# The rest of a low-rank product, repeated to 128 columns so that a gate's rows need no DRAM relay

## The chip, the cores and the metric

The kernel runs on one core of a Trainium2 chip. The metric is the device time of one execution in microseconds, as the median of several runs. The core has a matrix engine (TensorE, PE in the profile, with its weight loads shown as PEld), a vector engine (VectorE, DVE), a scalar engine (ScalarE, ACT), a general engine (GpSimd, POOL) and a queue processor (SyncE, SP) that issues all DMAs of this kernel. Each engine works through its own list of instructions in order and waits for others at semaphores.

## The reference

The reference is a transformer layer with self attention, cross attention and a feed-forward part, followed by one RWKV layer (time mixing with a recurrent state, then channel mixing). The input has 16 sequences of 256 tokens with 512 channels, all in float32. The change lies at the start of the time mixing:

```
xa = _ln(x, ln1_w, ln1_b)
sx = shift(xa) - xa
xxx = xa + sx * maa_x
t = tanh(xxx @ maa_w1).reshape(B, L, 5, 32)
m = einsum('blfd,fdc->blfc', t, maa_w2)
xw, xk, xv, xr, xg = (xa + sx * (maa_j + m[:, :, j]) for the five j)
```

`maa_w1` has 512 rows and 160 columns, which is five groups of 32. Each group of 32 tanh values is multiplied by its own 32 x 512 matrix, and the result blends the token with its predecessor, once for each of five uses: decay (w), key (k), value (v), receptance (r) and gate (g). The gate is the fifth.

## The kernel before

The kernel works in stages: self attention (A), cross attention (B), and then, for the sequences 0 to 7 and again for 8 to 15, a feed-forward stage (C) and a mix stage (D). The recurrence inside groups of eight tokens (I) runs beside the later stages, and the tail (E) carries the state, makes the outputs and does the channel mixing. One batch is one sequence of 256 tokens.

**The order.** The program is not issued as written. Each operation is recorded with the engine or engines that may do it, an assumed cost, and the tiles that it reads and writes (`emit`, `dma`). A list scheduler (`Sched.run`) then simulates engines with these costs, always takes the operation that could start first (ties by a priority made of the recording order and the table `PRIO`), and picks one of the allowed engines. So a small edit can change the order and the engine of operations far away. All DMAs are issued by SP, in the order found. Tiles live in a common pool: 34 slots of 4 KB per partition, each of which can hold one large tile or two small ones, and 4 blocks of 16 KB. For each stage `SIZES` says how many tiles of a tag may live at once, and tiles of one tag are given out in the order of recording. In the mix stage `xj`, the tiles of the blends, has three.

**Precise products.** Float32 values are split into a rounded part ("hi") and the remainder ("lo") by `split`: one copy by ScalarE or VectorE and one subtraction by VectorE or GpSimd. A large product is three matmuls per step: hi x hi, hi x lo and lo x hi (`mm3`, lines 486 to 488). The small product with `maa_w2` needs only one matmul, because the three terms are stacked along the contraction: 98 rows are 32 rows of hi, 32 of lo, 32 of hi again and two rows of ones that bring in `maa_j`. The weights `W2[j]` are stacked to match.

**The mix of one batch** (`mix`). `front` normalises, transposes and makes `xa`, `sx` and the first blend `xx`. `tmix` multiplies `xx` with `maa_w1`: 128 columns with the weights `W1` and the last 32 with `W1b`, 12 matmuls each, into the two halves of one PSUM bank. ScalarE applies tanh to both (line 1025), and both are split into the tile `th`. Now the 32 rows of each group, which stand in different partitions, have to be brought into partitions 0 to 97. This is done through DRAM, by the relay tensor `tdr`: two writes for the first four groups, one for the fifth, and then two reads into `S5` (four groups) and two into `S5b` (the fifth). The rows of ones are put into `tdr` once, in `mix_weights`. `blend(b, j)` then multiplies `W2[j]` with `S5` or, for j = 4, with `S5b` (line 1045), multiplies by `sx`, adds `xa` (lines 1050 and 1051) and splits the result into two `xj` tiles (lines 557 and 558). From these, `decay`, `rates`, `project` and `gate` make the five outputs. The recording order has `front` and `tmix` of the next batch beside the first two blends of this one, so the five groups of a batch are made most of a batch ahead of their use.

In `decay`, a similar stacked operand is made without DRAM: the weights `dw1` hold the 64 columns twice, so the product stands twice in 128 partitions, and the upper half is replaced by the remainder.

Of the kernel before, what the change touches and what calls it, by code (L numbers as in the profile page):

```python
# [9 lines left out]
F32R = mybir.dt.float32r  # L10
AF = mybir.ActivationFunctionType
# [9 lines left out]
def fv(ap):  # L21

    return ap.bitcast(F32)
# [368 lines left out]
class Kern:  # L392
# [505 lines left out]
class Rec(Kern):  # L898
# [14 lines left out]
    def mix_weights(self):  # L913

        nc, I, tile = self.nc, self.I, self.tile
        W1, W1b, dw1 = tile("W1", [128, 4, 2, 128], "W1", F32R), tile("W1b", [128, 4, 2, 32], "W1b", F32R), tile("dw1", [128, 4, 2, 128], "dw1", F32R)
# [14 lines left out]
        st, lo = tile("st", [128, 512], "st"), tile("st", [66, 512], "st2", F32R)  # L931
# [10 lines left out]
        self.tdr, self.t2l = [], []  # L942
        o1, o2 = tile("st", [66, 256], "ones"), tile("st", [66, 256], "ones2", F32R)
        self.dma(o1, lambda: o1[64:66], lambda: I["c_ones"], 2048)
        self.emit("DVE", c_dve(256), lambda: nc.vector.tensor_copy(out=o2[64:66], in_=o1[64:66]), [o1], [o2])
        for i in range(2):
            h = self.relay("tdr", [66, 5, 256], "tdr")
            self.dma(None, lambda h=h: h[64:66], lambda: fv(o2[64:66]).unsqueeze(1).to_broadcast([2, 5, 256]), 10240, r=[o2], w=[(h, 3)])
# [51 lines left out]
    def mix(self, src, rsrc, out, W, bs=range(B), side=None):  # L1000

        nc, tile, emit = self.nc, self.tile, self.emit
        W1, W1b, W2, dw1, D1, D2 = self.mixw
        st = {}
# [11 lines left out]
        def tmix(b):  # L1016
            xa, sx, xx = st[b]
            pt = tile("p_p", [128, 2, 256], "pt")
            xs = [lambda k=k: self.two(xx, k) for k in range(4)]
            self.mm3((pt, 0), lambda: pt[:, 0, :], [lambda k=k: (W1[:, k, 0, :], W1[:, k, 1, :]) for k in range(4)], xs, 256, [W1] + xx)  # L1020
            self.mm3((pt, 1), lambda: pt[0:32, 1, :], [lambda k=k: (W1b[:, k, 0, :], W1b[:, k, 1, :]) for k in range(4)], xs, 256, [W1b] + xx)
            T, th = tile("T", [128, 2, 256], "tt"), tile("xj", [128, 2, 2, 256], "th", F32R)
            dr, S5, S5b = self.tdr[b % 2], tile("S5", [98, 4, 256], "S5", F32R), tile("S5b", [98, 256], "S5b", F32R)
            for i, p in ((0, 128), (1, 32)):
                emit("ACT", c_act(256), lambda i=i, p=p: nc.scalar.activation(out=T[0:p, i, :], in_=pt[0:p, i, :], func=AF.Tanh), [(pt, i)], [(T, i)])
                self.split(256, lambda i=i, p=p: T[0:p, i, :], lambda i=i, p=p: th[0:p, i, 1, :], lambda i=i, p=p: th[0:p, i, 0, :], [(T, i)], (th, (i, 1)), (th, (i, 0)))
            for x in range(2):
                self.dma(None, lambda x=x: dr[32 * x : 32 * x + 32, 0:4, :].rearrange("d j n -> j d n"), lambda x=x: fv(th[:, 0, x, :]), 131072, [(th, (0, x))], [(dr, x)])
            self.dma(None, lambda: dr[0:64, 4, :].rearrange("(x d) n -> d x n", x=2), lambda: fv(th[0:32, 1, :, :]), 65536, [(th, (1, 0)), (th, (1, 1))], [(dr, 2)])
            self.dma(None, lambda: fv(S5[0:32]), lambda: dr[32:64, 0:4, :], 131072, [(dr, 1)], [(S5, 0)])  # L1030
            self.dma(None, lambda: fv(S5[32:98]), lambda: dr[0:66, 0:4, :], 66 * 4096, [(dr, 0), (dr, 1), (dr, 3)], [(S5, 1)])
# [85 lines left out]
        for i in range(5 * first, 5 * end):  # L1117
            b, j = divmod(i, 5)
# [115 lines left out]
class Tail(Rec):  # L1234
# [306 lines left out]
    "D": dict(wb=16, row=2, sm=4, st=4, x=1, xa=4, xx=2, W1=1, W1b=1, W2=5, dw1=1, dw2=2, t2l=2, T=3, xj=3, S5=2, S5b=2, s1=1, o=3, p_p=2, p_s=3, p_t=3, tdr=2),  # L1541
# [106 lines left out]
```

## Time and profile before

| what | us |
|---|---|
| median of 3 runs (lowest, highest) | 3563.89 (3561.29, 3566.48) |
| the profiled execution, its own time | 3571.95 |
| its span in the profile | 3570.2 |
| TensorE busy | 3273.7 |
| VectorE busy | 2843.3 |
| ScalarE busy | 1882.5 |
| GpSimd busy | 1395.8 |

The span runs from the first to the last instruction of the profiled execution. "Busy" counts the time in which an engine executes instructions; the ends of matmuls are modelled, so a busy TensorE need not be at its peak. Windows of the trace give the busy time of each engine in a stretch, and the clock that TensorE was granted there (1.00 is full). A row of the waits reads "who waited, for whose instruction": the engine, the tile it was about to write and the line, then the engine, tile and line that released it. Tiles from the common pool appear as slot, block or bank; buffers of the relay as tdr. A line can be that of a helper that many places call: 486 to 488 are all precise products, 472 all subtractions of `split` and `sub`, 461 all DMAs. The first mix stage is at about 1815 to 2140 us, the second at about 2460 to 2780 us, and the tail is from there to the end.

### The profile page before, as it was taken

The page shows a single profiled execution, that of the slowest core. Times are in us where ns is not written, and L with a number is a line of the kernel's source. Part 1 is how long each engine was busy: PE and PEld are TensorE (multiplying, and loading weights), DVE is VectorE, ACT ScalarE, POOL GpSimd, SP SyncE. Part 2 cuts the span into 40 slices and gives each one's busy share as a digit, 9 for nine tenths or more (in the row PEclk, how much of TensorE's full clock was granted, in tenths as well). Part 3 has the DMA queues.
Part 4 walks back from the last instruction along what each step waited for, and adds up shares of the span by engine and source line. Part 5 has one row for each costly group of instructions (what it writes and reads, how often), then busy time and mean ns, then how long its engine had stood idle before and what let it go on. Part 6 is the DMA issues. An engine that isn't in the chain of part 4 may idle for free. (4 is left out here: it accounts for less than half of the span.)

```text
span 3570.2 us, 72760 instructions
## 1 busy us (share of the span) xinstructions
PE 3273.7 (92%) x26978; PEld 2620.6 (73%) x26978; DVE 2843.3 (80%) x6696; ACT 1882.5 (53%) x4722; POOL 1395.8 (39%) x1853
## 2 busy tenths in 40 slices
PE   6999999989999999899999989999999558878899
PEld 4777877767777777788887879998787445555555
DVE  6888898868887788766788788899878688887653
ACT  4665666656666666433354454344444565554532
POOL 3444444444444444100021129994211476764110
PEclk9999999999999999899999999999999789998999
DMA  3111000021111110300134463343444877674420
GB/s 97 37 31 35 27 25 31 21 90 46 43 43 43 43 51 25 100 25 24 42 111 134 131 203 110 112 138 107 129 144 156 245 206 205 182 217 127 133 81 24
DMA packets 325051, 336.83 MB, mean 94 GB/s; under 512 B 40978, under 2 KB 228446, under 8 KB 324698
## 3 DMA queue, kind: packets, MB, share of 16 engines
q1 hardware_dynamic: 324698, 332.18, 30.5%
q8 instruction: 214, 3.51, 0.4%
q14 instruction: 139, 1.14, 0.1%
HBM read 199.92 MB, written 132.16 MB: 93 GB/s over the span
## 5 line engine op out<-in xcount | busy, mean ns | idle before, releaser
L721 POOL TENSOR_SCALAR slot<-slot,k_rin 128x256 f32<-128x256 f32 x1024 | 482.0, 488 | 691.8 <-DVE k_rin L718 624.8
L472 POOL TENSOR_TENSOR slot<-slot,slot 128x512 f32<-128x512 f32 (+9 forms) x394 | 540.4, 1393 | 312.7 <-ACT slot L551 133.2
L715 ACT ACTIVATE slot<-slot,k_nmx 128x256 f32<-128x256 f32 x1024 | 507.9, 498 | 199.3 <-DVE k_nmx L714 168.8
L486 PE MATMUL bank<-slot,block 128*128 128x256 f32 x1792 | 510.9, 285 | 0.2 <-ACT slot L467 0.2
L487 PE MATMUL bank<-slot,block 128*128 128x256 f32 x1792 | 508.0, 284 | 0.3 <-DVE slot L603 0.3
L488 PE MATMUL bank<-slot,block 128*128 128x256 f32 x1792 | 507.9, 283 | 0.0
L467 ACT ACTIVATE slot<-bank 128x512 f32<-128x512 f32 (+2 forms) x659 | 351.5, 565 | 270.4 <-PE bank L488 142.8
L486 PE MATMUL bank<-block,slot 128*128 128x512 f32 x1152 | 468.4, 407 | 11.3 <-ACT slot L557 10.2
L488 PE MATMUL bank<-block,slot 128*128 128x512 f32 x1152 | 453.8, 394 | 9.0 <-DVE slot L558 9.0
L487 PE MATMUL bank<-block,slot 128*128 128x512 f32 x1152 | 452.5, 393 | 0.0
L714 DVE CUSTOM_DVE_ANT_0 slot<-slot,slot 128x256 f32<-128x256 f32 x998 | 390.9, 436 | 0.0
L708 DVE SCALAR_TENSOR_TENSOR slot<-bank,slot 128x512 f32<-128x512 f32 x512 | 329.9, 680 | 44.3 <-PE bank L746 21.0
L1471 PE MATMUL bank<-block,slot 128*128 128x512 f32 x768 | 354.4, 613 | 1.6 <-DVE slot L1517 1.0
L486 PEld LDWEIGHTS bank<-slot,block 128*128 128x128 f32 x1792 | 344.1, 192 | 10.3 <-ACT slot L467 2.3
L487 PEld LDWEIGHTS bank<-slot,block 128*128 128x128 f32 x1792 | 344.0, 192 | 5.3 <-DVE slot L603 0.5
L488 PEld LDWEIGHTS bank<-slot,block 128*128 128x128 f32 x1792 | 344.1, 192 | 0.0
L487 PE MATMUL bank<-slot,slot 128*128 128x256 f32 (+2 forms) x960 | 309.1, 322 | 12.4 <-DVE slot L472 9.7
L486 PE MATMUL bank<-slot,slot 128*128 128x256 f32 (+2 forms) x960 | 307.9, 321 | 10.4 <-ACT slot L551 9.3
L734 PE MATMUL bank<-k_c,slot 128*128 128x128 f32 x2048 | 287.5, 281 | 25.1 <-POOL slot L721 10.9
L488 PE MATMUL bank<-slot,slot 128*128 128x256 f32 (+2 forms) x960 | 306.1, 319 | 1.5 <-DVE slot L558 1.5
L734 PEld LDWEIGHTS bank<-k_c,slot 128*128 128x128 f32 x2048 | 232.1, 143 | 96.3 <-POOL slot L721 64.1
L1471 PEld LDWEIGHTS bank<-block,slot 128*128 128x128 f32 x768 | 146.0, 196 | 168.6 <-issue 156.5
(195 smaller groups left out, 6639.3 us busy)
## 6 DMA issues: line engine op xcount, KB each, us to landing
slot<-in SPq DMA_DIRECT2D x153, 256.0 KB
slot<-x SPq DMA_DIRECT2D x64, 512.0 KB
x<-slot SPq DMA_DIRECT2D x48, 512.0 KB
slot<-in SPq DMA_DIRECT2D x32, 512.0 KB
sdr<-slot SPq DMA_DIRECT2D x128, 128.0 KB
slot<-sdr SPq DMA_DIRECT2D x32, 512.0 KB
s_k<-slot SPq DMA_DIRECT2D x16, 512.0 KB
s_w<-slot SPq DMA_DIRECT2D x16, 512.0 KB
```

Of the source, the lines that this page charges most:

```text
L467: self.emit(("ACT", "DVE"), (c_act(n), c_dve(n)), (lambda: nc.scalar.activation(out=out(), in_=in_(), func=AF.Copy), lambda: nc.vector.ten ...
L472: self.emit(("DVE", "POOL"), (c_dve(n), c_pool(n)), (lambda: nc.vector.tensor_tensor(out=out(), in0=in0(), in1=in1(), op=op), lambda: nc.g ...
L486: nc.tensor.matmul(o, lhsT=lh, rhs=rh, start=first and i == 0, stop=False)
L487: nc.tensor.matmul(o, lhsT=lh, rhs=rl, start=False, stop=False)
L488: nc.tensor.matmul(o, lhsT=ll, rhs=rh, start=False, stop=last and i == k - 1)
L708: emit("DVE", c_dve(512), lambda j=j, T=T: nc.vector.scalar_tensor_tensor(out=T(), in0=ps[j](), scalar=-scale, in1=mask(), op0=ALU.mult, o ...
L714: emit("DVE", c_dve(256) + 80, lambda T=T, j=j, qt=qt: nc.vector.tensor_tensor_reduce(out=T[:, qt, :], in0=T[:, qt, :], in1=negb[:, qt, :] ...
L715: emit("ACT", c_act(256, 1, 1), lambda T=T, Et=Et, j=j, qt=qt: nc.scalar.activation(out=Et[:, qt, :], in_=T[:, qt, :], func=AF.Exp, scale= ...
L721: emit("POOL", 470, lambda jj=jj, qt=qt: nc.gpsimd.tensor_scalar(out=E[jj][:, qt, :], in0=E[jj][:, qt, :], scalar1=rin[:, qt, jj : jj + 1] ...
L734: nc.tensor.transpose(pt[:, k, 128 * qt : 128 * qt + 128], E[j][:, qt, 128 * k : 128 * k + 128], self.ident())
L1471: self.nc.tensor.matmul(po(), lhsT=x[k // 2][:, k % 2, ts], rhs=w[k // 2][:, k % 2, :], start=k == 0, stop=k == 3)
```

## The change

The weights of the last 32 columns, `W1b`, become 128 columns wide and hold the 32 columns four times. The product then stands four times in 128 partitions. Tanh is taken on 96 of them. One copy brings all 96 rows, rounded, into `S5b`, and one subtraction overwrites rows 32 to 63 with the remainder. The rows of ones are written once into two lasting `S5b` tiles, `t4`. The write of the fifth group to `tdr` and its two reads go, and `tdr` has four groups in place of five. The tanh tile `th` now holds only the first 128 rows; it is half as large and has the tag `s1`, of which there are two in place of one, and no longer the tag `xj`.

```diff
-        W1, W1b, dw1 = tile("W1", [128, 4, 2, 128], "W1", F32R), tile("W1b", [128, 4, 2, 32], "W1b", F32R), ...
+        W1, W1b, dw1 = tile("W1", [128, 4, 2, 128], "W1", F32R), tile("W1b", [128, 4, 2, 128], "W1b", F32R), ...
...
-                self.split(4 * m, lambda st=st, o=o, m=m: st[:, :, o : o + m], lambda w=w: w[:, :, 0, :], lambda w=w: w[:, :, 1, :], [st], (w, 0), (w, 1))
+                rows = lambda w, x, m=m: w[:, :, x, :].rearrange("p k (r c) -> p k r c", c=m)
+                self.split(512, lambda st=st, o=o, m=m: st[:, :, o : o + m].unsqueeze(2).to_broadcast([128, 4, 128 // m, m]), lambda w=w, rows=rows: rows(w, 0), lambda w=w, rows=rows: rows(w, 1), [st], (w, 0), (w, 1))
...
+        o3 = tile("st", [98, 256], "ones3")
+        self.dma(o3, lambda: o3[96:98], lambda: I["c_ones"], 2048)
...
-            h = self.relay("tdr", [66, 5, 256], "tdr")
+            h = self.relay("tdr", [66, 4, 256], "tdr")
...
+            h = tile("S5b", [98, 256], f"S5b{i}", F32R)
+            self.emit("DVE", c_dve(256), lambda h=h: nc.vector.tensor_copy(out=h[96:98], in_=o3[96:98]), [o3], [(h, 2)])
+            self.t4.append(h)
...
-            self.mm3((pt, 1), lambda: pt[0:32, 1, :], [lambda k=k: (W1b[:, k, 0, :], W1b[:, k, 1, :]) for k in range(4)], xs, 256, [W1b] + xx)
-            T, th = tile("T", [128, 2, 256], "tt"), tile("xj", [128, 2, 2, 256], "th", F32R)
-            dr, S5, S5b = self.tdr[b % 2], tile("S5", [98, 4, 256], "S5", F32R), tile("S5b", [98, 256], "S5b", F32R)
-            for i, p in ((0, 128), (1, 32)):
+            self.mm3((pt, 1), lambda: pt[:, 1, :], [lambda k=k: (W1b[:, k, 0, :], W1b[:, k, 1, :]) for k in range(4)], xs, 256, [W1b] + xx)
+            T, th = tile("T", [128, 2, 256], "tt"), tile("s1", [128, 2, 256], "th", F32R)
+            dr, S5, S5b = self.tdr[b % 2], tile("S5", [98, 4, 256], "S5", F32R), self.t4[b % 2]
+            for i, p in ((0, 128), (1, 96)):
                 emit("ACT", c_act(256), lambda i=i, p=p: nc.scalar.activation(out=T[0:p, i, :], in_=pt[0:p, i, :], func=AF.Tanh), [(pt, i)], [(T, i)])
-                self.split(256, lambda i=i, p=p: T[0:p, i, :], lambda i=i, p=p: th[0:p, i, 1, :], lambda i=i, p=p: th[0:p, i, 0, :], [(T, i)], (th, (i, 1)), (th, (i, 0)))
+            self.split(256, lambda: T[:, 0, :], lambda: th[:, 1, :], lambda: th[:, 0, :], [(T, 0)], (th, 1), (th, 0))
...
-            self.dma(None, lambda: dr[0:64, 4, :].rearrange("(x d) n -> d x n", x=2), lambda: fv(th[0:32, 1, :, :]), 65536, [(th, (1, 0)), (th, (1, 1))], [(dr, 2)])
...
-            self.dma(None, lambda: fv(S5b[0:32]), lambda: dr[32:64, 4, :], 32768, [(dr, 2)], [(S5b, 0)])
-            self.dma(None, lambda: fv(S5b[32:98]), lambda: dr[0:66, 4, :], 66 * 1024, [(dr, 2), (dr, 3)], [(S5b, 1)])
+            emit(("ACT", "DVE"), (c_act(256) + 43, c_dve(256, 0, True)), (lambda: nc.scalar.activation(out=S5b[0:96], in_=T[0:96, 1, :], func=AF.Copy), lambda: nc.vector.tensor_copy(out=S5b[0:96], in_=T[0:96, 1, :])), [(T, 1)], [(S5b, 0), (S5b, 1)])
+            self.sub(256, lambda: S5b[32:64], lambda: T[32:64, 1, :], lambda: fv(S5b[32:64]), [(T, 1), (S5b, 0)], [(S5b, 1)])
...
-    "D": dict(..., S5=2, S5b=2, s1=1, ...),
+    "D": dict(..., S5=2, S5b=2, s1=2, ...),
```

More of the change, by code (lines that the diff above doesn't have):

```diff
@@ L915, in mix_weights @@
         nc, I, tile = self.nc, self.I, self.tile
-        W1, W1b, dw1 = tile("W1", [128, 4, 2, 128], "W1", F32R), tile("W1b", [128, 4, 2, 32], "W1b", F32R), tile("dw1", [128, 4, 2, 128], "dw1", F32R)
+        W1, W1b, dw1 = tile("W1", [128, 4, 2, 128], "W1", F32R), tile("W1b", [128, 4, 2, 128], "W1b", F32R), tile("dw1", [128, 4, 2, 128], "dw1", F32R)
         for src, n, ws in ((I["L1_xattn_maa_w1"], 160, ((W1, 0, 128), (W1b, 128, 32))), (I["c_dw1"], 128, ((dw1, 0, 128),))):
@@ L941, in mix_weights @@
         self.mixw = W1, W1b, W2, dw1, D1, D2
-        self.tdr, self.t2l = [], []
+        self.tdr, self.t2l, self.t4 = [], [], []
+        o3 = tile("st", [98, 256], "ones3")
+        self.dma(o3, lambda: o3[96:98], lambda: I["c_ones"], 2048)
         o1, o2 = tile("st", [66, 256], "ones"), tile("st", [66, 256], "ones2", F32R)
@@ L946, in mix_weights @@
         for i in range(2):
-            h = self.relay("tdr", [66, 5, 256], "tdr")
-            self.dma(None, lambda h=h: h[64:66], lambda: fv(o2[64:66]).unsqueeze(1).to_broadcast([2, 5, 256]), 10240, r=[o2], w=[(h, 3)])
+            h = self.relay("tdr", [66, 4, 256], "tdr")
+            self.dma(None, lambda h=h: h[64:66], lambda: fv(o2[64:66]).unsqueeze(1).to_broadcast([2, 4, 256]), 8192, r=[o2], w=[(h, 3)])
             self.tdr.append(h)
@@ L1027, in tmix @@
             for x in range(2):
-                self.dma(None, lambda x=x: dr[32 * x : 32 * x + 32, 0:4, :].rearrange("d j n -> j d n"), lambda x=x: fv(th[:, 0, x, :]), 131072, [(th, (0, x))], [(dr, x)])
-            self.dma(None, lambda: dr[0:64, 4, :].rearrange("(x d) n -> d x n", x=2), lambda: fv(th[0:32, 1, :, :]), 65536, [(th, (1, 0)), (th, (1, 1))], [(dr, 2)])
-            self.dma(None, lambda: fv(S5[0:32]), lambda: dr[32:64, 0:4, :], 131072, [(dr, 1)], [(S5, 0)])
-            self.dma(None, lambda: fv(S5[32:98]), lambda: dr[0:66, 0:4, :], 66 * 4096, [(dr, 0), (dr, 1), (dr, 3)], [(S5, 1)])
@@ L1032, in tmix @@
-            self.dma(None, lambda: fv(S5b[0:32]), lambda: dr[32:64, 4, :], 32768, [(dr, 2)], [(S5b, 0)])
-            self.dma(None, lambda: fv(S5b[32:98]), lambda: dr[0:66, 4, :], 66 * 1024, [(dr, 2), (dr, 3)], [(S5b, 1)])
+                self.dma(None, lambda x=x: dr[32 * x : 32 * x + 32, :, :].rearrange("d j n -> j d n"), lambda x=x: fv(th[:, x, :]), 131072, [(th, x)], [(dr, x)])
+            emit(("ACT", "DVE"), (c_act(256) + 43, c_dve(256, 0, True)), (lambda: nc.scalar.activation(out=S5b[0:96], in_=T[0:96, 1, :], func=AF.Copy), lambda: nc.vector.tensor_copy(out=S5b[0:96], in_=T[0:96, 1, :])), [(T, 1)], [(S5b, 0), (S5b, 1)])
@@ L1034, in tmix @@
+            self.sub(256, lambda: S5b[32:64], lambda: T[32:64, 1, :], lambda: fv(S5b[32:64]), [(T, 1), (S5b, 0)], [(S5b, 1)])
+            self.dma(None, lambda: fv(S5[0:32]), lambda: dr[32:64], 131072, [(dr, 1)], [(S5, 0)])
+            self.dma(None, lambda: fv(S5[32:98]), lambda: dr[0:66], 66 * 4096, [(dr, 0), (dr, 1), (dr, 3)], [(S5, 1)])
             st[b][2] = S5, S5b
@@ L1540 @@
     "C": dict(wb=16, w=16, row=2, cf=1, sm=4, st=8, x=2, xh=2, xT=2, E=4, PT=1, cT=1, p_p=2, p_s=3, p_t=3),
-    "D": dict(wb=16, row=2, sm=4, st=4, x=1, xa=4, xx=2, W1=1, W1b=1, W2=5, dw1=1, dw2=2, t2l=2, T=3, xj=3, S5=2, S5b=2, s1=1, o=3, p_p=2, p_s=3, p_t=3, tdr=2),
+    "D": dict(wb=16, row=2, sm=4, st=4, x=1, xa=4, xx=2, W1=1, W1b=1, W2=5, dw1=1, dw2=2, t2l=2, T=3, xj=3, S5=2, S5b=2, s1=2, o=3, p_p=2, p_s=3, p_t=3, tdr=2),
     "E": dict(wb=8, sm=4, st=2, x=3, xx=8, T=4, T4=2, s0=2, Y=2, rp=1, gt=1, uc=2, d0=2, Sc=2, tot=1, gs=2, KB=3, KBc=1, SBc=1, SB=4, VO=2, RP=4, p_p=2, p_u=2, p_y=2, p_t=2, d_s=2),
```

## The prediction

> **What bounds the kernel now.** I read the page's head first, then TensorE's idle time by stage (windows), then its waits in the two mix stages, one batch of the mix in order of time, and last the tail stage.
>
> ```profile
> span 3570.2 us, 72760 instructions
> PE 3273.7 (92%) x26978; PEld 2620.6 (73%) x26978; DVE 2843.3 (80%) x6696; ACT 1882.5 (53%) x4722; POOL 1395.8 (39%) x1853
> PE   6999999989999999899999989999999558878899
> ```
>
> TensorE is busy for 92% of the span, so most stages end when its matmuls do. The slices with 5 and 8 (from about 2760 us) are the tail. The mix runs twice, at 1815 to 2140 and at 2460 to 2780 us. Ten-microsecond windows of one batch of it (PE, PEld, DVE, ACT, POOL busy, then clock and DMA):
>
> ```profile
> 1930.00:1940.00 10.00, 10.00 (x75) 9.53 (x74) 5.17 (x8) 3.64 (x7) 0.00 (x0) 1.00 0.48 146
> 1940.00:1950.00 10.00, 7.26 (x44) 5.76 (x43) 9.90 (x19) 4.88 (x10) 3.64 (x5) 0.94 0.16 54
> 1950.00:1960.00 10.00, 10.00 (x49) 8.32 (x48) 7.95 (x18) 6.13 (x12) 1.63 (x2) 0.89 0.23 63
> ```
>
> A batch alternates: a stretch bound by TensorE (10.00, VectorE only 5.17), then one bound by VectorE (9.90), in which TensorE loses 2.74 us and the granted clock falls for a moment (0.94, then 0.89). What TensorE waits for in the first mix stage (us in total, times, longest):
>
> ```profile
> PE bank L486 <- ACT slot L557: 10.0, 2, 9.8
> PE bank L488 <- DVE slot L558: 4.6, 7, 1.2
> PE bank L487 <- DVE slot L472: 4.4, 5, 0.9
> PE bank L486 <- ACT slot L551: 4.2, 5, 0.9
> PE bank L1045 <- DMA slot<-tdr: 1.6, 1, 1.6
> ```
>
> The reader should see that the relay (tdr) is one wait of 1.6 us, before the first batch. The 10.0 us stand at the change to the next stage. The three rows between, 13.2 us, are the splits that VectorE and ScalarE make for the blends. The second mix stage has the same rows with 5.9, 5.3 and 5.1 us and again 1.6 us for tdr.
>
> Now the parts that the change touches, in order of time:
>
> ```profile
> 1878.91 0.28 PE L488 MATMUL bank<-slot,slot 128*128 128x256 f32 x1
> 1879.03 0.28 PE L486 MATMUL bank<-slot,slot 128*128 128x256 f32 x1
> 1880.33 0.11 PEld L486 LDWEIGHTS bank<-slot,slot 128*32 128x32 f32 x1
> 1880.33 0.28 PE L488 MATMUL bank<-slot,slot 128*32 128x256 f32 x1
> 1880.44 0.28 PE L486 MATMUL bank<-slot,slot 128*32 128x256 f32 x1
> 1882.21 2.90 SPq L461 DMA_DIRECT2D tdr<-slot  x3
> 1887.93 1.67 SPq L461 DMA_DIRECT2D slot<-tdr  x2
> 1932.72 0.64 PE L1045 MATMUL bank<-slot,slot 98*128 98x256 f32 x4
> ```
>
> **The change part by part.** *The wider product.* 12 matmuls a batch get 128 columns of weights in place of 32. The moving side stays 256 columns, so the pitch of starts decides: 0.120 us in the 128-wide group (1878.91 to 1879.03), 0.1164 us in the 32-wide one (12 starts from 1879.75 to 1881.03). The difference, 0.0036 us x 12 x 16 batches = +0.7 us, lies on TensorE's path; it cannot be under 0, nor much over 0.08 us a matmul (the two loads' difference), +15. The 32-wide load is 0.11 us long, the 128-wide load has a median of 0.192 us; both start while the matmul before still runs.
>
> The Trainium skill, "TensorE: Matmul & The Clock Gate", LDWEIGHTS (loading the stationary operand), speaks against this part: a load's time goes with its columns, about P/1.2 ns, so 27 ns becomes 107 ns. If that difference lay open it would be, as an estimate from that page, 80 ns x 192 = +15 us; the two pitches above say that it is hidden, and the sum goes by them.
>
> *The relay that goes.* Three DMAs a batch go (one write of 64 KB, reads of 32 and 66 KB), 48 in all, with about 0.7 us of SP each (2.90 us for three, 1.67 for two). SP is in order; behind them stand the stores of k, w and v. I cost this at nothing: the batch's last two reads start at 1887.93 and its fifth blend, which alone uses them, runs at 1932.72, 43 us after the reads are issued. That cover is the work of a whole batch; were it gone, a batch would pay the distance from tanh (1881.35) to the reads' issue (1889.6), 8 us. The other four rows still go through DRAM, so the 1.6 us waits before the two first batches stay, at most shortened: 0 to -3.2 us, taken -0.5, since the large transfers remain ahead.
>
> *The rows written directly.* One copy of 96 rows and one subtraction of 32 rows replace one copy and one subtraction of 32 rows. These go by elements per row, 256 in both (0.42 and 0.41 us before), so 0. The third row block holds tanh twice over: tanh on 96 rows also takes 256 elements, 0.36 us.
>
> *Preparation.* The repeated weights are split over 512 elements and not 128, twice per stage, and four copies of two constant rows (0.28 us each) and one small load per stage come in: about +2 us on VectorE and ScalarE in the feed-forward stages, where TensorE has 10.00 of 10 us. Cost 0; without that cover +2.
>
> *Buffers and order.* The tanh tile leaves the ring of three blend tiles. The recorder orders everything by its own costs, so the built programs differ far beyond the edit. Compared instruction by instruction, TensorE's order in a settled mix batch is the same, and so is VectorE's from the fifth blend to the mix product, which is the stretch with 9.90; only the third blend's split moves up, into a stretch where TensorE has 10.00. Over both mix stages VectorE loses 7 normalising scalings (0.54 us), 5 subtractions of the small blend (0.68), 3 copies (0.68) and 3 shifts, some 11 us, to ScalarE and GpSimd. Bounds: -11 us if all of it lies in the full stretches, and +4 us, since three of the subtractions now take 1.29 us on GpSimd (0.68 before) ahead of the product that waits for them, twice over. As the settled batches keep their order, I take -2.
>
> *The tail.* The same work in another order: VectorE has 10 operations fewer, ScalarE 12 fewer, GpSimd 22 more (spreads at 0.69 us, copies at 0.61, products at 1.3: about +16 us), 18 state products stand before the first output product (14 before), and four weight tiles are loaded before the state inputs instead of among them. Windows of 30 us:
>
> ```profile
> 2780.00:2810.00 30.00, 12.38 (x225) 11.34 (x223) 15.66 (x29) 13.88 (x34) 4.56 (x5) 0.76 0.92 273
> 2870.00:2900.00 30.00, 12.88 (x180) 9.37 (x179) 27.61 (x53) 14.44 (x34) 17.09 (x15) 0.66 0.66 179
> 3140.00:3170.00 30.00, 23.58 (x448) 14.82 (x450) 25.48 (x39) 18.63 (x47) 27.83 (x22) 0.89 0.73 199
> 3470.00:3500.00 30.00, 30.00 (x99) 17.11 (x98) 15.17 (x38) 8.88 (x16) 3.68 (x7) 1.00 0.05 18
> ```
>
> From 2780 to 3260 us no engine is full throughout; DMA (0.92) and then VectorE (27.61) come last; after 3440 us it is TensorE alone. Bounds from its idle rows: -25 us, if most of the 13.1 and 16.6 us waits there (for state inputs at 2819 and for VectorE at 2890) go; +27, if one more of 16.6 us and one like the 10.0 us above arise. The sum of work hardly moves, so I take 0.
>
> Sum: 0.7 - 0.5 - 2 + 0 = -1.8 us against the profiled execution's 3571.95 us (its span is 3570.2), so 3570.2. That execution is 8.06 us above the median of 3563.89; the same step on the median is 3562.
>
> **The rivals.**
> *Slower by the tail's order.* GpSimd's extra 16 us fall where VectorE is full, and they slow it:
>
> ```profile
> 2846.63 0.23 DVE L1441 TENSOR_TENSOR k_gt<-k_gt,k_gr 128x64 f32<-128x64 f32 x1
> 2883.58 5.05 POOL L472 TENSOR_TENSOR slot<-slot,slot 128x512 f32<-128x512 f32 x4
> 2886.19 1.32 DVE L1441 TENSOR_TENSOR k_gt<-k_gt,k_gr 128x64 f32<-128x64 f32 x1
> ```
>
> The same 64-element step took 0.23 us alone and 1.32 us beside a GpSimd product. Six such steps in one normalisation are about 6 us; two to three more hits, plus a few us of GpSimd's own queue, give +14: 3578. It decides once more than 7 us of it reach TensorE. Against it: from 3440 us on TensorE is full, and delay that leaves it fed is lost.
>
> *Slower in the mix.* The small blend's subtraction on GpSimd delays the product in all 16 batches by 0.6 us: +10, 3574. For it: the waits on L472; against: it is moved in three cases.
>
> *Faster.* All 11 us of VectorE's relief count and the weight loads no longer delay the state inputs (13.1 us wait, half gone): -18, 3546. For it: DMA at 0.92 there; against: SP must issue the same number of loads.
>
> *The relay was on the path.* Excluded by the 43 us above for all but the first batches.
>
> **How the numbers follow.** 0.2% is 7.1 us, about what a measurement can tell from no change. Forecast (within it) 0.37; slower by the tail 0.25 and by the mix 0.10; faster 0.28. So faster 0.28, same 0.37, slower 0.35. The forecast's own range is 3557 to 3571. Two in ten left out, the range is 3540 to 3590: down to most of the gain bound of the tail with the relief, up to the tail's +27.
>
> **What would show it.** Right: no 32-column weight load at 0.11 us and a pitch of 0.120 us in both groups; tdr with 32 reads and about 36 writes; mix windows that still fall to about 7.3 with VectorE at 9.9; TensorE's waits on tdr still near 1.6 us twice. Wrong: a mix batch shorter or longer than now by over 0.3 us, or windows from 2780 to 3260 us in which TensorE's sum differs by over 7 us; then the tail's order and not the edit sets the time.

## The result: 1% slower, with the loss in the tail

The changed kernel takes 3601.82 us (median of 4 runs, 3599.13 to 3603.94). Its ratio to the kernel before, which took 3563.14 us in the same comparison, is 1.0103 with a 95% interval of 1.0089 to 1.0118. The forecast was 3562 us with a range up to 3590: no change was expected, and the result lies outside the range.

The head of the page after, and TensorE's busy share in 40 slices:

```profile
span 3598.7 us, 72691 instructions
PE 3289.3 (91%) x26978; PEld 2633.3 (73%) x26978; DVE 2840.1 (79%) x6680; ACT 1880.2 (52%) x4718; POOL 1411.7 (39%) x1877
PE   6999999989999999899999989999998368879899
```

Up to the second mix the slices are as before; the tail begins with 3 and 6, where it had 5 and 5. Landmarks say where the profiled executions part. SyncE issues one store of the gate (s_g) per mix batch, so the first and the last of them bound the two mix stages, and what is left of the span behind the last one is the tail. SyncE's queue of the changed kernel (start, time, line, transfer):

```profile
1871.33 0.36 SPq L461 DMA_DIRECT2D s_g<-slot  x1
...
2789.61 0.38 SPq L461 DMA_DIRECT2D s_g<-slot  x1
...
2992.77 0.38 SPq L461 DMA_DIRECT2D out_dram<-slot  x1
```

The same for the kernel before:

```profile
1869.17 0.36 SPq L461 DMA_DIRECT2D s_g<-slot  x1
...
2789.11 0.40 SPq L461 DMA_DIRECT2D s_g<-slot  x1
...
2970.76 0.45 SPq L461 DMA_DIRECT2D out_dram<-slot  x1
```

| profiled execution, us | before | after | difference |
|---|---|---|---|
| to the first s_g store | 1869.2 | 1871.3 | +2.1 |
| first mix, first to eighth store | 249.7 | 248.6 | -1.1 |
| between the mixes | 419.2 | 419.9 | +0.7 |
| second mix | 251.0 | 249.8 | -1.2 |
| tail, last s_g store to the end | 781.1 | 809.1 | +28.0 |

At the last mix store the two kernels stand within 0.5 us of each other; the first result is stored 22 us later, the last one 28 us. The two profiled executions differ by 28.5 us, the medians by 38.7: the profiled execution of before stood 8.8 us above the median of this comparison, that of after 1.4 us below. So the table places 28.5 us of the loss, and not the 10 us beyond them.

TensorE's matmuls in the tail, by line and shape, kernel before (busy us, mean ns of one, then idle time ahead of them with its causes):

```profile
L1471 PE MATMUL bank<-block,slot 128*128 128x512 f32 x768 | 354.4, 613 | 1.6 <-DVE slot L1517 1.0 <-DVE slot L472 0.3 <-POOL slot L472 0.2
L1512 PE MATMUL bank<-slot,block 128*128 128x256 f32 x512 | 115.6, 384 | 0.8 <-DVE slot L1429 0.4 <-DVE slot L1366 0.4
L1397 PE MATMUL bank<-k_c,slot 128*128 128x128 f32 x128 | 18.3, 292 | 0.0
```

The same three groups in the changed kernel, whose lines are five higher:

```profile
L1476 PE MATMUL bank<-block,slot 128*128 128x512 f32 x768 | 361.0, 623 | 14.7 <-DVE slot L1522 6.1 <-DVE slot L1434 4.2 <-DVE slot L1290 2.4
L1517 PE MATMUL bank<-slot,block 128*128 128x256 f32 x512 | 120.3, 395 | 3.9 <-DVE slot L1434 3.9
L1402 PE MATMUL bank<-k_c,slot 128*128 128x128 f32 x128 | 17.8, 283 | 25.1 <-ACT slot L1306 25.1
```

In these three groups the idle time grows by 41 us; in the other four large groups of the tail it shrinks by 28 (the heads' from 54.1 to 36.2 us, that of L593 from 23.5 to 4.0). Over all seven, idle time goes from 141.4 to 154.7 us, and the busy time of the same matmuls from 679.8 to 694.0. So about half of the 28 us is waiting, and the other half is the same matmuls at a lower granted clock. The trace's record of the clock confirms the second half: in the tail it stands at 0.50 for 195 us, before for 154, and 123.5 us of TensorE's busy time fall there, before 90.5. Counting busy time at 0.50 as half, the work is 593 us in both kernels. Both halves can be read beside the longest wait of the changed kernel. TensorE's own order there (in brackets the idle time ahead, and what ended it):

```profile
2782.74 1.04 PE L1402 MATMUL bank<-k_c,slot 128*128 128x128 f32 x8
...
2886.89 1.97 PE L1402 MATMUL bank<-k_c,slot 128*128 128x128 f32 x8 [25.14 <-ACT slot L1306]
```

Two windows of the changed kernel (busy time of PE, PEld, DVE, ACT and POOL with their instructions, then the granted clock, the DMA share and GB/s):

```profile
2862.00:2886.00 24.00, 0.00 (x0) 0.00 (x0) 5.65 (x9) 0.80 (x2) 13.32 (x9) 0.57 0.91 249
2885.00:2890.00 5.00, 3.11 (x15) 3.11 (x16) 0.42 (x1) 3.00 (x10) 2.67 (x3) 0.50 0.95 267
```

After 25 us without a matmul the clock is 0.50, and eight transposes take 1.97 us where they took 1.04 before. The Trainium skill, "TensorE: Matmul & The Clock Gate", section HAM oscillation — how this bites in real kernels, says that an idle gap of over about 3.4 us lets the clock fall to half, so that the matmuls behind it start slow. This wait agrees: the clock falls 3.5 us after its start, and the rows behind it have 0.50 and 1.97 against 1.04. But shorter gaps were enough elsewhere in this tail: it has 26 spells at 0.50 ahead of the last matmul, and only 12 idle gaps of over 3.4 us.

Windows that answer to those shown of the tail before:

```profile
2780.00:2810.00 30.00, 10.25 (x169) 9.26 (x167) 16.98 (x22) 13.52 (x39) 11.07 (x8) 0.73 0.77 235
2870.00:2900.00 30.00, 11.37 (x155) 7.82 (x156) 10.54 (x25) 10.00 (x28) 19.98 (x14) 0.57 0.68 194
3140.00:3170.00 30.00, 16.75 (x402) 12.11 (x400) 21.91 (x30) 19.87 (x49) 21.71 (x17) 0.72 0.83 235
3470.00:3500.00 30.00, 30.00 (x99) 17.19 (x98) 13.78 (x32) 9.82 (x17) 3.69 (x7) 1.00 0.17 54
```

At 2870 us VectorE is no longer full (10.54 in place of 27.61): it waits too. At 3470 us TensorE is alone again, as before.

The mix, in windows that answer to those of before:

```profile
1930.00:1940.00 10.00, 10.00 (x62) 8.99 (x61) 4.36 (x7) 2.95 (x6) 0.00 (x0) 1.00 0.58 181
1940.00:1950.00 10.00, 7.84 (x56) 6.69 (x54) 8.72 (x16) 6.03 (x13) 2.35 (x4) 1.00 0.24 83
1950.00:1960.00 10.00, 9.83 (x49) 8.75 (x50) 9.21 (x19) 4.28 (x10) 2.94 (x3) 0.83 0.08 21
```

The mix alternates between TensorE and VectorE as it did, and the relay has two writes and two reads per batch:

```profile
1884.47 1.54 SPq L461 DMA_DIRECT2D tdr<-slot  x2
1887.84 2.14 SPq L461 DMA_DIRECT2D slot<-tdr  x2
```

### The profile page after: what moved, and what is told of

Read it like the earlier page. It is cut to its first block, busy times and chain, and to the rows that moved or that the text cites. A ratio compares the mean times of both kernels' runs of the same rounds, so it can differ in the third digit from the quotient of the medians.

```text
span 3598.7 us, 72691 instructions
## 1 busy us (share of the span) xinstructions
PE 3289.3 (91%) x26978; PEld 2633.3 (73%) x26978; DVE 2840.1 (79%) x6680; ACT 1880.2 (52%) x4718; POOL 1411.7 (39%) x1877
## 5 line engine op out<-in xcount | busy, mean ns | idle before, releaser
L486 PE MATMUL bank<-slot,slot 128*128 128x256 f32 (+1 forms) x960 | 307.9, 321 | 14.3 <-ACT slot L551 9.4
L487 PE MATMUL bank<-slot,slot 128*128 128x256 f32 (+1 forms) x960 | 309.0, 322 | 12.4 <-DVE slot L472 9.7
L734 PE MATMUL bank<-k_c,slot 128*128 128x128 f32 x2048 | 287.3, 281 | 25.1 <-POOL slot L721 10.2
L488 PE MATMUL bank<-slot,slot 128*128 128x256 f32 (+1 forms) x960 | 306.3, 319 | 0.9 <-DVE slot L558 0.8
```

The lines of the kernel that those rows point to most:

```text
L486: nc.tensor.matmul(o, lhsT=lh, rhs=rh, start=first and i == 0, stop=False)
L487: nc.tensor.matmul(o, lhsT=lh, rhs=rl, start=False, stop=False)
L488: nc.tensor.matmul(o, lhsT=ll, rhs=rh, start=False, stop=last and i == k - 1)
L734: nc.tensor.transpose(pt[:, k, 128 * qt : 128 * qt + 128], E[j][:, qt, 128 * k : 128 * k + 128], self.ident())
```

## The experiments

The suspicion after this result was that the edit costs nothing and that the planner's new order of the tail is the loss: the tail's 2870 operations (state pass and output stage) are the same in both kernels, but they are differently ordered, and 254 of them run on another engine. The rival was the edit itself. All ratios below are to the kernel before in the same comparison, where its median was 3566.6 to 3569.1 us; 0.1% is 3.6 us.

For these runs the planner follows a given sequence instead of its own cost rule. It keeps its rules for memory, and may still put a tile into another slot. The common edit (the list is a rank and an engine for each operation):

```diff
-        engs = sorted({a[0] for o in ops for a in o.alts})
+        engs = follow(ops) or sorted({a[0] for o in ops for a in o.alts})
...
-                    kx = (s, o.prio, a[1])
+                    kx = (o.prio, s, a[1])
...
+    for o, r, c in zip(ops, rank.tolist(), raw[2 * n :]):
+        o.prio, o.alts = r, [a for a in o.alts if a[0] == ("PE", "ACT", "DVE", "POOL", "SP")[c]]
```

**The whole order exchanged.** First the edit in the order of before. Its new operations stand beside those that they replace, and the rule that keeps room for earlier stages had to go:

```diff
-        kept = sum(sum(d.values()) for p, d in self.reserve[sp].items() if p < h.phase)
+        kept = 0
...
+ORDER = (
...
```

> The whole edit (128-wide small product, tanh on 96 rows, fifth blend from there without the relay), but every operation that both kernels have is issued in the order, and on the engine, of the kernel before; TensorE's and GpSimd's orders are the same throughout, the tail's order on every engine too. Theory (the loss of 38.7 us is the order that the planner gives the tail; the edit itself is worth about nothing): 3563 us, between 3556 and 3570, the first store of the result again near 2971 us and no wait of TensorE for ScalarE's copy of the 25.1 us kind in the tail. Rival (the edit itself costs it: wider weight loads, lost cover, more work on GpSimd): 3595 to 3605 us.

Then the kernel before in the order of the changed one, relay and all; the edit is the common one:

```diff
-                    kx = (s, o.prio, a[1])
+                    kx = (o.prio, s, a[1])
...
+ORDER = (
...
```

> The operations of the kernel before, relay and 32-wide product included, in the order and on the engines of the changed kernel; the tail's order is that of the changed kernel on every engine, the mix has some small moves on VectorE and ScalarE. Theory (the tail's order): 3595 to 3608 us, with the 25.1 us wait of TensorE for the copy of the third rp load, near 2886 us. Rival (the edit itself): 3556 to 3570 us.

Measured: 1.0066 (1.0052 to 1.0079), 3590.87 us, for the edit in the old order; 1.0122 (1.0108 to 1.0136), 3609.77 us, for the relay in the new order. The second is what the theory says: without the edit, the order alone loses as much as the changed kernel, with its wait:

```profile
2893.95 1.33 PE L1397 MATMUL bank<-k_c,slot 128*128 128x128 f32 x5 [25.81 <-ACT slot L1301]
```

The first is neither 3563 nor 3600. Its first s_g store comes at 1883.2 us, 14 us late, and between the mixes it loses 6 us more: the two handovers from the feed-forward stage, where the memory rule was off. Its mixes take 248.6 and 252.6 us, and its tail 791.7 us, 11 more than before although the order is the old one. (The profiled execution was the slowest of the five, 12 us above their median.) So this run cannot tell what the edit costs.

**One load.** The 25.1 us wait ends when ScalarE has copied the third rp load, which stands in SyncE's queue 71 places behind its place in this edit (rows of SyncE's order):

```diff
+L461 DMACopy slot_30763<-s_rp 128x2x512
...
 L461 DMACopy slot_31236<-s_v 128x8x128
-L461 DMACopy slot_31240<-s_rp 128x2x512
```

> The changed kernel in its own order, but for one DMA: the third rp load of the tail is issued 71 places earlier in SyncE's queue, ahead of the first v load of the output stage. Nothing else is moved. Theory (one late load in SyncE's queue is the larger part of the loss): TensorE's 25.1 us wait goes to under 5 us, and as other stretches of the tail keep their order, 15 to 25 us come off the end: 3577 to 3587 us. Rival (the wait is only where a delay shows that VectorE or GpSimd make anyway): under 7 us come off, 3595 to 3602 us, and a wait of about the same length stands soon behind for another engine.

And in the kernel before, one load later (the fifth rp load, which stands where the late one of the changed kernel does):

```diff
-L461 DMACopy slot_30828<-s_rp 128x2x512
...
 L461 DMACopy s_rp<-slot_30442 1024x1x128
+L461 DMACopy slot_31268<-s_rp 128x2x512
```

> The kernel before in its own order, but for one DMA: the fifth rp load of the tail is issued 43 places later in SyncE's queue, behind the first store of rp by the output stage, where the changed kernel has its late one. Nothing else is moved. Theory (a late load in SyncE's queue delays the tail to its end): 10 to 25 us slower, 3573 to 3588 us. Rival (the tail absorbs a late load, since TensorE alone sets the end from 3440 us): within 7 us of 3563.

Measured: 1.0095 (1.0079 to 1.0112) with the load early, 3 us better than the changed kernel, and 1.0005 (0.9996 to 1.0014) with the load late. The theory of the one load falls. The waits of TensorE with the load early show why (window from 2780 to 2990 us; us in total, times, longest):

```profile
PE bank L1431 <- DVE slot L1413: 21.9, 5, 18.7
...
PE bank L1402 <- ACT slot L1306: 4.3, 3, 2.7
```

The 25.1 us are gone from the copy and stand 18.7 us long at the next step of the same batch. VectorE has the copy for that step (L1413) behind other work that is not ready. A reduction of the recurrence (L1189) waits 13.0 us for a product of GpSimd, which itself waits 10.6 us for a load of s_k issued at 2872 us; a reduction of the next starting states (L1332) waits for a load issued at 2882 us. VectorE's order there:

```profile
2880.43 0.69 DVE L1189 TENSOR_REDUCE slot<-slot 128x32 f32<-128x512 f32 x1 [13.02 <-POOL slot L472]
...
2888.28 0.42 DVE L1332 TENSOR_REDUCE k_sm<-slot 128x16 f32<-128x256 f32 x1 [4.33 <-DMA slot<-in]
2888.73 2.44 DVE L1413 COPY slot<-bank 32x128 f32<-32x128 f32 x8
```

So the batch stands late in every queue, and not in SyncE's alone.

**The tail exchanged alone.** What the new order does in the first third of the tail is best seen on TensorE. In the orders as built, R stands for the read-out transposes of a batch (from its rp load), S for its state products (four groups; in brackets how many), H for its heads (line 1426 of before) and O for its output product. Where two steps run into each other, as S1 and R2 or H3 and O1 do in the kernel after, one is put ahead of the other:

```
before  R1 R2 S1 S2 H1 S3(2) R3 S3(2) S4(1) H2 S4(1) R4 O1 S4(2) H3 S5(2)
after   R1 R2 S1 S2 H1 S3 H2 S4 S5(2) R3 H3 O1 R4
```

The changed kernel runs the state ahead, up to the fifth batch, and comes to the third batch's read-out and the first output product later. Now all stages ahead of the tail keep their own order, and the 2870 operations of the tail fill the places of the tail in the order, and on the engines, of the other kernel (the same edit as above, with another list). The changed kernel with the tail of before, as TensorE's order:

```diff
-R1 R2 S1 S2 H1 S3 H2 S4 S5(2) R3 H3 O1 R4
+R1 R2 S1 S2 H1 S3(2) R3 S3(2) S4(1) H2 S4(1) R4 O1 S4(2) H3 S5(2)
```

> The changed kernel, with the mix and all stages ahead of it in its own order; only the operations of the tail (state pass and output stage, 2870 of them, the same in both kernels) are put in the sequence, and on the engines, that they have in the kernel before. Theory (the tail's order is the whole loss, and the edit with its handovers costs nothing): 3556 to 3572 us on a chip whose kernel before takes 3563 to 3569, the first store of the result near 2971 us. Rival (the edit itself costs some of it, as the run with the whole order of before left 22 us): 3582 to 3595 us.

The kernel before with the tail of the changed one:

```diff
-R1 R2 S1 S2 H1 S3(2) R3 S3(2) S4(1) H2 S4(1) R4 O1 S4(2) H3 S5(2)
+R1 R2 S1 S2 H1 S3 H2 S4 S5(2) R3 H3 O1 R4
```

> The kernel before, relay and 32-wide product in place and the mix in its own order; only the 2870 operations of the tail are put in the sequence, and on the engines, of the changed kernel. Theory (the tail's order): 3595 to 3612 us. Rival (the edit): 3556 to 3572 us.

Measured: 1.0032 (1.0020 to 1.0045), 3580.37 us, and 1.0135 (1.0121 to 1.0149), 3616.77 us. The order of the tail gives back 25 of the changed kernel's 37 us, and costs the kernel before 48. Of these 48, the tail itself takes 29 (810.3 us); the rest is a seam, since the last stores of the mix, about 36 us apart before, are now 42 and 50 apart. Some 11 us of the changed kernel's loss are left even with the tail of before; in its profiled execution the tail takes 789.8 us, 9 more than in the kernel before.

**Sequence and engines.** In four runs the kernel before keeps all work, and only engines or sequence of the tail change. The edit of the first, as rows of GpSimd's order (excerpt):

```diff
-L1364 TensorCopy slot_30435<-slot_29895 128x512
 L1291 TensorScalarPtr slot_30493<-slot_30433,k_em 128x32x16
...
+L1364 TensorCopy slot_30503<-slot_29895 128x512
...
+L1291 TensorScalarPtr slot_30573<-slot_30433,k_em 128x32x16
```

> The kernel before in its own sequence, but 254 small operations of the tail (copies, spreads, products) run on the engine that the changed kernel gives them, so GpSimd has 22 more there. Theory (the sequence of the tail's batches makes the loss, not the choice of engines): within 8 us of the kernel before. Rival (the forecast's own: GpSimd's added work and its slowing of VectorE's short operations): 10 to 25 us slower.

The sequence of the changed kernel, the engines of before:

```diff
-R1 R2 S1 S2 H1 S3(2) R3 S3(2) S4(1) H2 S4(1) R4 O1 S4(2) H3 S5(2)
+R1 R2 S1 S2 H1 S3 H2 S4 S5(2) R3 H3 O1 R4
```

> The kernel before; the tail's operations in the sequence of the changed kernel, but each on the engine that it has in the kernel before. Theory (sequence and engines add up: 48 us for both, some 18 for the engines alone): 25 to 36 us slower than before, ratio 1.007 to 1.010. Rival (the engines were chosen for their own sequence, so either half alone is worse than the pair): 48 us or more, ratio 1.013 and above.

Of the engines, only what concerns GpSimd:

```diff
-L1364 TensorCopy slot_27311<-slot_29895 128x512
...
+L1364 TensorCopy slot_27311<-slot_29895 128x512
...
+L1291 TensorScalarPtr slot_30573<-slot_30433,k_em 128x32x16
```

> The kernel before in its own sequence; of the 254 operations of the tail that change engine only the 122 that go to GpSimd (72) or leave it (50) are changed; the swaps between VectorE and ScalarE are left out. Theory (GpSimd's added work makes the engines' share): 10 to 22 us slower, ratio 1.003 to 1.006. Rival (the swaps between VectorE and ScalarE make it): under 7 us, ratio below 1.002.

And less work for GpSimd than before:

```diff
-L1364 TensorCopy slot_30370<-slot_29895 128x512
-L1364 TensorCopy slot_27311<-slot_29895 128x512
-L1364 TensorCopy slot_30435<-slot_29895 128x512
-L1291 TensorScalarPtr slot_30493<-slot_30433,k_em 128x32x16
```

> The kernel before in its own sequence; 39 operations of the tail that GpSimd has (15 copies of the decay at 0.64 us, 24 spreads of the keys at 0.7 us, about 26 us of GpSimd) go to ScalarE. Theory (GpSimd's work in the tail costs time by itself): 3 to 15 us faster, ratio 0.996 to 0.999, which would beat both kernels. Rival (any move away from the planned engines loses, whichever way): slower by 3 us or more, ratio above 1.001.

| kernel before, its tail with | ratio | interval |
|---|---|---|
| the engines of after | 1.0047 | 1.0032 to 1.0063 |
| the sequence of after | 1.0188 | 1.0173 to 1.0204 |
| both | 1.0135 | 1.0121 to 1.0149 |
| GpSimd's part of the engines | 1.0031 | 1.0019 to 1.0043 |
| 39 operations off GpSimd | 1.0011 | 1.0001 to 1.0022 |

The two halves do not add up: the sequence alone costs 67 us, with its own engines 48. The engines of the new plan fit its sequence and not the other one. The moves that concern GpSimd (72 operations onto it, 50 off it) cost 11 us in the old sequence; but taking work off GpSimd gains nothing there either (4 us slower).

**Where in the tail.** The changed kernel with the first 528 operations of the tail as before, and then with the other 2342 (both by lists, with the common edit). The first brings the old order of TensorE back where it was shown, and leaves the rest:

```diff
-R1 R2 S1 S2 H1 S3 H2 S4 S5(2) R3 H3 O1 R4
+R1 R2 S1 S2 H1 S3(2) R3 S3(2) S4(1) H2 S4(1) R4 O1 S4(2) H3 S5(2)
```

> The changed kernel; of its tail only the first 528 operations (those that both kernels have in the first third of the tail, up to about the third stored result) are put in the sequence and on the engines of the kernel before; the other 2342 keep those of the changed kernel. The changed sequence runs four more state products ahead of the third batch's read-out (five rp loads are issued by 2831 us in the kernel before, two in the changed one). Theory (that batch's late read-out, not one load of it alone, is the larger part of the loss): the first store is back near 2975 us and 15 to 28 us come off the changed kernel, ratio to the kernel before 1.002 to 1.006. Rival (the loss is spread over the tail): the first store is back, but the lead is gone by the end, ratio 1.008 to 1.011.

The second keeps this part and changes what follows:

```diff
+ORDER = (
...
```

> The changed kernel; of its tail the first 528 operations keep their sequence and engines, and the other 2342 get those of the kernel before: the complement of the run in which the first 528 were exchanged and gave back 9 us. Theory (the loss is spread, so each part gives back its share): 12 to 20 us off the changed kernel, ratio to the kernel before 1.004 to 1.007. Rival (the two parts only fit together, and neither gives back anything alone): ratio 1.009 or more.

Measured: 1.0078 (1.0063 to 1.0092) and 1.0119 (1.0105 to 1.0133), where the whole tail gave 1.0032 and none 1.0103. The first third gives back 9 us, the rest alone gives back nothing, and together they give 25. With the first third exchanged, TensorE's 25.1 us wait is gone, and one of before is back (2780 to 2990 us):

```profile
PE bank L1364 <- DMA block<-s_v: 46.9, 6, 14.9
PE bank L593 <- DVE slot L472: 16.4, 1, 16.4
```

So the loss can't be put down to a place in the tail, any more than to one load.

**Other plans of the same work.** Four kernels whose plan differs for a reason that has nothing to do with the work. The kernel before, with room for 128 columns where 32 are used:

```diff
-        W1, W1b, dw1 = ..., tile("W1b", [128, 4, 2, 32], "W1b", F32R), ...
+        W1, W1b, dw1 = ..., tile("W1b", [128, 4, 2, 128], "W1b", F32R), ...
...
-                self.split(4 * m, ..., lambda w=w: w[:, :, 0, :], lambda w=w: w[:, :, 1, :], ...)
+                self.split(4 * m, ..., lambda w=w, m=m: w[:, :, 0, 0:m], lambda w=w, m=m: w[:, :, 1, 0:m], ...)
```

> The kernel before with one number changed: the tile of the small product's weights is given room for 128 columns, of which 32 are used as before. No work is added or taken away; the planner, which places tiles by the room that is free, orders the rest anew. Theory (any new order of the tail is worse than the one the kernel has, so a new plan by itself loses): 8 to 40 us slower. Rival (the loss needs the edit's own operations): within 7 us.

The kernel before, with tanh assumed 5 ns dearer:

```diff
-                emit("ACT", c_act(256), lambda i=i, p=p: nc.scalar.activation(out=T[0:p, i, :], ...
+                emit("ACT", c_act(256) + 5, lambda i=i, p=p: nc.scalar.activation(out=T[0:p, i, :], ...
```

> The kernel before, its work unchanged; only the planner's assumed cost of tanh is 5 ns higher, which gives a new order in and behind the first mix stage (the tail: mean move 5.4 places on SyncE, 5.3 on VectorE). Theory (any new plan of the tail loses): 6 to 30 us slower, ratio 1.002 to 1.008. Rival (new plans go both ways about the old one): ratio below 1.001.

The changed kernel with a ring of three tanh tiles, and with four blend tiles:

```diff
-    "D": dict(..., xj=3, S5=2, S5b=2, s1=2, ...),
+    "D": dict(..., xj=3, S5=2, S5b=2, s1=3, ...),
```

> The changed kernel with one number changed: the ring of the tanh tile has three places, not two. The work is the same; the planner's tail comes out as in the run of the kernel before with room for 128 columns (10 moves of 2870), whose tail took 784 us from the last mix store to the end, against 781 in the kernel before and 809 in the changed one. Theory (the plan of the tail is the loss, and the edit is worth about nothing): 16 to 30 us off the changed kernel, ratio to the kernel before 1.001 to 1.006. Rival (the edit's own operations cost it): ratio 1.009 or more.

```diff
-    "D": dict(..., xj=3, S5=2, S5b=2, s1=2, ...),
+    "D": dict(..., xj=4, S5=2, S5b=2, s1=2, ...),
```

> The changed kernel with one number changed: four blend tiles, not three, which gives another plan again with the same work; on SyncE the tail is nearer to that of the kernel before (mean move 5.6 places, 8.1 in the changed kernel). Theory (the plan): ratio 1.000 to 1.007, below the changed kernel's 1.0103. Rival (the edit): 1.009 or more.

| plan | ratio | interval | tail, us |
|---|---|---|---|
| before, room for 128 columns | 1.0037 | 1.0023 to 1.0051 | 783.5 |
| before, tanh + 5 ns | 0.9996 | 0.9987 to 1.0005 | 781.8 |
| after, three tanh tiles | 1.0022 | 1.0013 to 1.0031 | 785.0 |
| after, four blend tiles | 1.0074 | 1.0055 to 1.0093 | 792.2 |
| after | 1.0103 | 1.0089 to 1.0118 | 809.1 |

One number more in a table of ring sizes, with the edit untouched, takes 24 us of its tail away:

```profile
span 3577.3 us, 72636 instructions
...
2792.26 0.45 SPq L461 DMA_DIRECT2D s_g<-slot  x1
```

This shows that the tail's plan and not the edit is the bulk of the loss. The tail is not the only stage that a plan moves: with four blend tiles 441.7 us lie between the mixes, 22 more than before, and with room for 128 columns the first s_g store comes 9 us late and the time between the mixes is 7 us longer, so most of these two losses stands ahead of the tail. The tail of the kernel with three tanh tiles is still not free of late loads (waits of TensorE from 2780 to 2990 us):

```profile
PE bank L1364 <- DMA block<-s_v: 22.9, 4, 13.9
PE bank L1402 <- ACT slot L1306: 11.6, 1, 11.6
```

And the expectation that any new plan loses fell: the one with the dearer tanh, which moves the tail's operations by 5 places on average on SyncE and VectorE, loses nothing. Plans differ by up to 1%, and which one comes out hangs on numbers that have nothing to do with the tail.

**The edit ahead of a good tail.** Last, the tail of the plan with the dearer tanh behind the changed mix:

```diff
+ORDER = (
...
```

> The changed kernel, with the mix and all ahead of it in its own order; the tail's 2870 operations in the sequence, and on the engines, of the run in which the kernel before was planned with a tanh 5 ns dearer (tail 781.8 us from the last mix store, ratio 0.9996). Theory (the plan of the tail is the whole loss, and the edit is worth 0 within 0.2%): ratio 0.999 to 1.003, tail 780 to 787 us. Rival (the edit takes something from any tail behind it, as the 11 us that were left with the tail of the kernel before): ratio 1.003 to 1.006, tail 788 us or more.

Measured: 1.0035 (1.0024 to 1.0047), tail 793.0 us; the rival's numbers. Four tails have now been run behind both kernels (ratios of the whole time):

| tail planned for | ahead of it the relay | ahead of it the edit |
|---|---|---|
| before | 1.0000 | 1.0032 |
| before, tanh + 5 ns | 0.9996 | 1.0035 |
| after | 1.0135 | 1.0103 |
| room for 128 columns; three tanh tiles (10 moves apart) | 1.0037 | 1.0022 |

In the first three rows the kernel for which the tail was not planned is 0.3 to 0.4% slower, whichever of the two that is; in the fourth, where each kernel has planned it for itself, the edit is not behind, and the two tails take 783.5 and 785.0 us. That reads as a plan that fits the moment at which the mix hands over its buffers, and not as a cost of the edit; but it is only argued. No run takes the handover apart from the rest, or from the slots that the planner chose anew, and a cost of the edit of up to some 0.3% is not excluded.

## Why the prediction was wrong

*The wider product*: right. The second group follows the first without a step, 0.120 us from start to start:

```profile
1881.79 0.28 PE L488 MATMUL bank<-slot,slot 128*128 128x256 f32 x1
1881.91 0.28 PE L486 MATMUL bank<-slot,slot 128*128 128x256 f32 x1
```

Over all 24 matmuls of this batch the mean pitch is 0.1196 us, some 0.003 us above the 0.1164 of the narrow group; 0.0036 was summed. The weight loads of the second group went from 0.136 to 0.20 us (means over the mix), and next to none of that shows in the pitch. The rule of the Trainium skill, "TensorE: Matmul & The Clock Gate", LDWEIGHTS (loading the stationary operand), that a load's time goes with its columns, does not fit: by these means four times the columns take 1.5 times as long.

*The relay that goes*: right. TensorE's only wait on tdr is 0.8 us, once, in place of 1.6 us twice, which is 2.4 us where 0.5 were taken, inside the bounds.

*The rows written directly*: right (tanh on 96 rows 364 ns, before 357 on 32; the copy 418 ns, before 417). The subtraction of 32 rows takes 0.42 us on VectorE and 0.73 on GpSimd, as it did before.

*Preparation* and *Buffers and order* in the mix: right in size. To the first store +2.1 us, where 0 stood, or +2 without cover; the two mixes -2.3 us together, where the steps in the mix sum to -1.8. TensorE's waits for GpSimd's subtractions in the mixes stay at 0.9 and 1.8 us (before 0.9 and 1.7), so the rival "Slower in the mix" did not come about. The kernel before in the new order also has mixes of 247.8 and 249.7 us with its relay in place, so even these 2 us need not be the edit's.

*The tail*: here it failed. The step took 0 with bounds of -25 and +27, "the sum of work hardly moves, so I take 0". It measured +28.0 us, 1 us beyond its bounds. The work did stay the same; but up to 3260 us no engine is full throughout, as the step itself said, so the sum of work does not price this stretch. What counts there is how the batches mesh over the queues of five engines: in the runs here the same 2870 operations took from 781 to 824 us. The bounds also counted TensorE's waits alone, while half of the 28 us is matmuls at a lower granted clock.

*The rival "Slower by the tail's order"* had place and sign, at a chance of 0.25, and half the size (+14). Its mechanism did not show in this kernel. The short VectorE operations which GpSimd was to slow took 47.5 us in all in the tail, after 58.3 before; 14 of these 176 operations overlapped a product on GpSimd, before 18. GpSimd's added work does cost 11 us when it is put into the old sequence, and there the short operations take 62.0 us; whether that is the reason, no run shows.

*The test that was named* worked: from 2780 to 3260 us TensorE's busy time is 341.7 us in all, where it was 358.8; the difference of 17 is over the 7 that were to mean "the tail's order and not the edit sets the time".

*The level*: 10 of the 38.7 us on the medians are no step of the sum. The profiled execution of before, against which the sum was made, stood 8.8 us above its median in this comparison (8.1 above the one that the forecast used), and that of after 1.4 us below; "the same step on the median" took the two offsets to be equal.

What stays open: which moves of the new sequence make its tail slow. It is not the one load that was moved, and neither the first third, nor the rest, nor the choice of engines makes the loss by itself.

## What to carry to other kernels

Where a planner orders the whole program from assumed costs and ring sizes, an edit changes two things, its own work and the plan of everything behind it. Here the first is worth less than can be told apart from the plan (some 0.3%), and the second up to 1%, most of it in a stage that the edit does not touch. Read the new order of each stage that no single engine bounds, and when it differs, take the spread of such plans as the uncertainty of the forecast, on top of the sum of the steps. Before judging the edit, run it under two or three plans (one more ring place, a cost a few ns higher); when a wait in such a stage is traced to one load, look at what stands behind it on the other queues, since moving the load alone moved the wait by one step.

## What was not expected of the hardware

The added waiting of TensorE came with about as much again: half of the 28 us was idle time, and the other half the same matmuls at a lower granted clock (0.57 in the long wait, 0.50 just behind it; eight transposes in 1.97 us in place of 1.04). The prediction counted waits in its bounds once.

A single DMA that was issued 32 us later (the fifth rp load at 2863 us, before at 2831) left the time where it was, 1.0005, although the load that was late in the changed kernel (another batch's) had looked like the cause of its longest wait.
